# A message-passing layer on one core: nodes laid out in blocks of 49 to a partition, the list of edges packed in another order

## The chip, the cores and the metric

The kernel runs on one core of a Trainium2 chip. A core has five engines with an instruction queue each: TensorE (PE, matmuls; its weight loads are PEld), VectorE (DVE), ScalarE (ACT), GpSimd (POOL) and SyncE (SP, which issues DMAs). Transfers are carried by 16 DMA engines. They can be issued by SyncE and ScalarE, and by GpSimd where rows are gathered by an index. The metric is the time of one execution on the device in microseconds, lower is better.

## The reference

There are 6,250 nodes with 64 features each (`x`) and 206,250 edges sorted by their destination `dst`, each with a source node `src` and 64 features of its own (`edge_attr_64`).

```python
h = jnp.maximum(_layernorm(x, axis=-1), 0.0)
msg = h[src] + edge_attr_64
agg = jax.ops.segment_sum(msg, dst, num_segments=6250)
y = jax.nn.relu(agg @ W1 + b1) @ W2 + b2
return x + y
```

## The kernel before

**Two ways to sum over edges.** Of 202 tiles of 1,024 edges the rows of the first GA = G - GP = 178 are never gathered. For them the kernel counts how often source s occurs among the edges of each destination, and multiplies the normalized features `h` by these counts. A source is split into a low part, 0 to 127, and a high part, 0 to 48. A slot of three destinations holds up to 128 edges; `count` (L704) builds one-hot matrices `hot_lo` and `hot_key` on VectorE, one matmul (L720) makes the 128 x 147 counts, ScalarE writes them to SBUF (L722), and `product` (L750) multiplies them by `h3`, which is `h` in three bf16 parts (L755 for two of them, L758 for the third). Partition and column of `x` in SBUF (`xl`, L146) must match the low and high part of a source: `xl[lo, hi]` is the row of that node. The features of the edges themselves are summed by `chunk_sum` (L407), for all tiles but the last GP = 24. For these 24 tiles GpSimd gathers rows of `h` from a DRAM copy, `table`, adding them to the edges' features (`pfeat`), 8 gathers to a tile, and `sum_groups` (L440) sums both.

**The head of the program.** Instructions are issued in an order written out by hand (L134), so each engine runs them in the order of the text.

- x is loaded in three parts by SyncE (L151), then the last 106 rows (L152). Node n sits in partition n mod 128, column n // 128.
- The source list (L140) is made float by ScalarE (L242), turned by TensorE into rows of edges (`turn_src`, L245), and copied to `srcl` as integers. The list of destinations `dstn` is loaded by ScalarE's queue (L243).
- From every 256th destination (`firsts_i`, L138) comes for each slot the row of 256 edges in which it begins (`row_i`, L258). `fetch_row` (L275) gathers that row on GpSimd, four at a time in flight; `seek` (L279) finds the place in it on ScalarE; `place` (L285) makes the edge's number on VectorE.
- `norm_mean` (L461), `norm_center`, `norm_var` and `norm_root` are the layer norm on VectorE with squares on ScalarE, in three parts of 16, 16 and 17 columns.
- L561 packs destination and source into one word; L564 stores the list to DRAM (`packed`). `fetch_pair` (L541) gathers 129 words from there for each of 256 slots, `unpack` (L587) takes them apart, `turn` (L600) turns them into `keys`, from which counting starts.
- `norm_h` (L492) makes `h` and stores it to `table`. Row r of the table is lo * 49 + hi, so the sources of the last 24 tiles are converted by `table_rows` (L521), three instructions on VectorE.

**The main loop.** 22 blocks of 84 slots, 14 steps each. `before` (L894) names what is put in ahead of a step, besides counting and multiplying: the parts of `norm_b` and `norm_c` that finish `h3`, clearing of `sums`, further `fetch_row`, `seek` and `place`. `queue` and `pool_until` (L853) spread the gathers on GpSimd over the steps by a planned cost of each. After the loop (L1029 on) stand the last multiplications, the last groups of gathered tiles and the stores of `out_y`.

Of the kernel before, what the change touches and what calls it, by code (L numbers as in the profile page):

```python
# [9 lines left out]
F32 = mybir.dt.float32  # L10
BF16 = mybir.dt.bfloat16
I32 = mybir.dt.int32
I16 = mybir.dt.int16
AF = mybir.ActivationFunctionType
OP = mybir.AluOpType
# [92 lines left out]
def gnn_kernel(ctx: ExitStack, tc: tile.TileContext, x, src_t, dst_t, dst_g, edge, w1, b1, w2, b2, out):  # L108
# [31 lines left out]
    nc.scalar.dma_start(src, src_t[:, :GA * J])  # L140
    dstn = pr.tile([QA, 2, P * J], I32, name="dstn")

    firstp_i = small.tile([1, GP], I32, name="firstp_i")
    nc.scalar.dma_start(firstp_i.rearrange("o (q h k) -> o q h k", h=2, k=1),
                        dst_g[GA // 2:G // 2, :, 0:1].unsqueeze(0))
    xl = consts.tile([P, HI + 1, D], F32, tag="x", name="xl")  # L146
    nc.gpsimd.memset(xl[:, HI - 1, :], 0.0)
    thirds = [(0, 16), (16, 32), (32, HI)]
    for h0, h1 in thirds:
        h1 = min(h1, HI - 1)  # L150
        nc.sync.dma_start(xl[:, h0:h1, :], x[h0 * P:h1 * P, :].rearrange("(h l) d -> l h d", l=P))  # L151
    nc.sync.dma_start(xl[:N % P, HI - 1, :], x[N - N % P:, :])  # L152

# [59 lines left out]
    for q in range(JQ):  # L213
# [25 lines left out]
    nc.vector.tensor_tensor(less, rest.unsqueeze(2).to_broadcast([P, NR, P]),  # L239
                            iota_v.unsqueeze(1).to_broadcast([P, NR, P]), op=OP.is_lt)  # L240
    srcf = src.bitcast(F32)
    nc.scalar.activation(srcf, src, AF.Copy)  # L242
    nc.scalar.dma_start(dstn, dst_g[:QA])  # L243

    def turn_src(h):  # L245
        pt = ps.tile([P, J, P], F32, tag="pc", name="psrc")
        for j in range(J):
            nc.tensor.transpose(pt[:GA // 2, j, :], srcf.rearrange("p (q h j) -> p q h j", h=2, j=J)[:, :, h, j], ident)
        nc.scalar.activation(srcl[:GA // 2, h].rearrange("q p j -> q j p"), pt[:GA // 2], AF.Copy)

    turn_src(0)
    pf = ps.tile([P, IC], F32, tag="po", name="pf", bufs=1)
# [22 lines left out]
    def fetch_row(i):  # L275
        rows_of[i] = small.tile([P, L1], I32, name="rows", bufs=4)
        gather(rows_of[i], dst_g.rearrange("q h (r k) -> (q h r) k", k=L1), row_i[:, i:i + 1])

    def seek(i0, n):  # L279
        for i in range(i0, i0 + n):  # L280

            inrow = small.tile([P, L1], BF16, name="inrow", bufs=2)
            nc.scalar.activation(inrow, rows_of[i], AF.Sign, bias=nhalf[:, i:i + 1], accum_out=first[:, i, 1:2])  # L283

    def place(i0, n):  # L285
        to = first[:, i0:i0 + n, 0]
        nc.vector.scalar_tensor_tensor(to, first[:, i0:i0 + n, 1], -0.5, middle[:, i0:i0 + n],  # L287
                                       op0=OP.mult, op1=OP.add)
        nc.vector.tensor_scalar(first_i[:, i0:i0 + n], to, float(EA), None, op0=OP.min)
# [230 lines left out]

    def table_rows(index, tmp):  # L521

        nc.vector.tensor_scalar(tmp, index, LO_BITS, None, op0=OP.logical_shift_right)
        nc.vector.tensor_scalar(index, index, P - 1, None, op0=OP.bitwise_and)
        nc.vector.scalar_tensor_tensor(index, index, float(HI), tmp, op0=OP.mult, op1=OP.add)

    def find_groups():
# [18 lines left out]
    for i in range(4):  # L546
        fetch_row(i)
    turn_src(1)
    firstp = small.tile([1, GP], F32, name="firstp")
# [9 lines left out]
    norm_means()  # L559
    for h in range(2):  # L560
        nc.vector.scalar_tensor_tensor(dstn[:, h], dstn[:, h], DST_BITS,  # L561
                                       srcl[:QA, h].rearrange("q p j -> q (p j)"),
                                       op0=OP.logical_shift_left, op1=OP.bitwise_or)
    nc.scalar.dma_start(packed.rearrange("(q k) o -> q (k o)", q=QA), dstn.rearrange("q h k -> q (h k)"))  # L564
    seek(0, 3)
    for i in range(4, 7):
        fetch_row(i)
    place(0, 3)
    fetch_pair(0)
    for k in range(3):  # L570
        norm_center(k)
        if k < 2:
            seek(3 + 2 * k, 2)
    norm_var(0)
    norm_var(1)
    place(3, 4)
    fetch_pair(2)
    norm_var(2)
# [290 lines left out]
    chunk_starts(0, 2 * RC, "pc", 2)  # L869
    src_hi = late.tile([P, NWIN + NX], BF16, tag="part", name="src_hi").bitcast(I32)[:, :GP * J]  # L870
    table_rows(src_p, src_hi)
    unpack_pair(0)
# [18 lines left out]
    def then(k, f):  # L891
# [4 lines left out]
        2: [lambda: [fetch_h(g) for g in range(GA, GA + 4)], lambda: chunk_turn(0)],  # L896
        3: [lambda: open_pv(0, True), lambda: rows_later(7, 11)],
        16: [lambda: seek(9, 2), lambda: rows_later(11, IC)],
        18: [lambda: place(7, 4)],
        7: [lambda: norm_b(0)],  # L900
        9: [lambda: norm_b(1)],
        11: [lambda: norm_b(2)],
        15: [lambda: seek(7, 2), find_groups, lambda: norm_c(0), lambda: clear(0, 5)],
        17: [lambda: norm_c(1), lambda: clear(1, 5)],
# [180 lines left out]
    with tc.If(odd > 0):  # L1085
# [20 lines left out]
        with tc.For_i(0, G, 1) as g:  # L1106
# [6 lines left out]
            nc.sync.dma_start(index, src_t[:, ds(g * J, J)])  # L1113
            index_hi = work.tile([P, J], I32, name="index_hi", bufs=1)
            table_rows(index, index_hi)
            dst_1 = work.tile([P, J], I32, name="dst_1", bufs=1)
# [61 lines left out]
```

## Time and profile before

| | us |
|---|---|
| runs shown: median (lowest, highest) | 533.04 (532.72, 538.49) |
| the profiled execution | 525.21 |
| its span, first to last instruction | 523.4 |
| busy in the span: PE, PEld | 451.5, 385.6 |
| busy: DVE, ACT, POOL | 417.4, 360.1, 415.7 |
| mean granted TensorE clock | 0.974 |

The costliest groups of instructions (line, engine, operation, output and inputs, count; busy us, mean ns of one; idle time just before them and what ended it):

```profile
L267 POOL DMA_INDIRECT pfeat<-table,src_p x192 | 363.5, 1893 | 58.5 <-issue 54.9
L722 ACT ACTIVATE counts<-pc 128x882 bf16<-128x882 f32 x310 | 276.8, 908 | 41.0 <-PE pc L720 27.0
L720 PE MATMUL pc<-hot_key,hot_lo 128*128 128x147 bf16 x1860 | 175.1, 231 | 24.2 <-DVE hot_key L712 17.5
```

And the busy share of the DMA engines and what they moved, in 40 slices of 13.1 us:

```profile
DMA  9819812566577766654666676676577676676610
GB/s 203 211 42 329 220 29 39 146 172 156 117 171 179 167 171 181 171 138 95 161 162 155 149 178 153 140 184 163 129 173 175 137 198 146 141 192 164 155 14 14
```

A digit is a busy share in tenths. The first three slices are the head of the program: loads of x and of the lists in the first two, the steps between packing and counting in the third. Counting starts in the fourth. "Idle before" counts waiting ahead of a group; it costs time only on the engine that sets the end.

### The profile page before, as it was taken

How to read it: one execution, taken by the hardware profiler on the slowest of the kernel's cores; microseconds unless marked ns; L12 is line 12 of the kernel's file. 1: busy time of each engine (PE TensorE's matmuls, PEld its weight loads, DVE VectorE, ACT ScalarE, POOL GpSimd, SP SyncE). 2: the span in 40 equal slices, each digit the busy share in tenths (PEclk: the TensorE clock that was granted, in tenths of full speed). 3: DMA queues.
4: the chain of work that ended last, by engine and by line, in shares of the span. 5: the costliest groups of instructions: out<-in, count | busy, mean ns of one | idle time of the engine just before them, and what ended most of it. 6: DMA issues, size and time to landing. Idle time of an engine off the chain costs nothing. (4 is left out here: it accounts for less than half of the span.)

```text
span 523.4 us, 19099 instructions
## 1 busy us (share of the span) xinstructions
PE 451.5 (86%) x8183; PEld 385.6 (74%) x8184; DVE 417.4 (80%) x618; ACT 360.1 (69%) x534; POOL 415.7 (79%) x265
## 2 busy tenths in 40 slices
PE   3026767999699999988999999999999999999954
PEld 3015555888588888777888888888888888888743
DVE  5589986889699989988898978888879888879210
ACT  5246898778467767896777777777777777768300
POOL 6358888888888868888889888888888888888840
PEclk9999899999799999999999999999999999999977
DMA  9819812566577766654666676676577676676610
GB/s 203 211 42 329 220 29 39 146 172 156 117 171 179 167 171 181 171 138 95 161 162 155 149 178 153 140 184 163 129 173 175 137 198 146 141 192 164 155 14 14
DMA packets 118152, 78.78 MB, mean 151 GB/s; under 512 B 39096, under 2 KB 113326, under 8 KB 117870
## 3 DMA queue, kind: packets, MB, share of 16 engines
q1 hardware_dynamic: 88458, 64.95, 42.7%
q0 software_dynamic: 29200, 10.25, 16.7%
q10 hardware_dynamic: 404, 2.30, 1.5%
q8 instruction: 66, 1.08, 0.9%
q14 instruction: 24, 0.20, 0.1%
HBM read 73.48 MB, written 3.99 MB: 148 GB/s over the span
## 5 line engine op out<-in xcount | busy, mean ns | idle before, releaser
L267 POOL DMA_INDIRECT pfeat<-table,src_p x192 | 363.5, 1893 | 58.5 <-issue 54.9
L722 ACT ACTIVATE counts<-pc 128x882 bf16<-128x882 f32 x310 | 276.8, 908 | 41.0 <-PE pc L720 27.0
L720 PE MATMUL pc<-hot_key,hot_lo 128*128 128x147 bf16 x1860 | 175.1, 231 | 24.2 <-DVE hot_key L712 17.5
L712 DVE TENSOR_TENSOR hot_lo<-iota_lo,keys 128x1536 bf16<-128x1536 bf16 x155 | 148.0, 955 | 46.5 <-PE pc L720 46.0
L720 PEld LDWEIGHTS <-hot_lo 128*128 128x128 bf16 x1860 | 135.3, 100 | 47.7 <-DVE hot_key L712 22.3
L712 DVE TENSOR_TENSOR hot_key<-iota_key,keys 128x1776 bf16<-128x1776 bf16 x155 | 167.1, 1078 | 0.0
L755 PE MATMUL pv<-counts,h 128*128 128x252 bf16 (+1 forms) x1078 | 149.6, 273 | 0.1
L755 PEld LDWEIGHTS <-h 128*128 128x128 bf16 x1078 | 99.2, 98 | 8.7 <-issue 0.4
L758 PE MATMUL pv<-counts,h 128*64 128x252 bf16 (+1 forms) x1078 | 78.0, 280 | 0.0
L407 PE MATMUL bank<-feat,hot 128*21 128x64 f32 x3168 | 59.0, 223 | 1.5 <-DMA feat<-in_edge 0.8
L410 ACT ACTIVATE by_node<-bank 128x128 f32<-128x128 f32 x66 | 18.4, 278 | 60.8 <-PE bank L407 60.7
L758 PEld LDWEIGHTS <-h 128*64 128x64 bf16 x1078 | 55.3, 113 | 4.4 <-issue 0.8
L407 PEld LDWEIGHTS bank<-feat,hot 128*21 128x21 f32 x3168 | 47.4, 102 | 14.8 <-issue 9.5
L395 DVE TENSOR_TENSOR hot<-rel,iota 128x504 f32<-128x504 bf16 x66 | 44.6, 677 | 0.6 <-PE bank L407 0.6
L267 POOL DMA_INDIRECT rows<-in_dst_g,row_i x15 | 18.6, 1238 | 14.9 <-ACT inrow L283 7.9
L267 POOL DMA_INDIRECT words<-packed,first_i x15 | 19.5, 1302 | 4.6 <-issue 3.4
L419 PE MATMUL pv<-select,by_node 128*64 128x42 f32 x264 | 21.2, 244 | 0.4 <-ACT by_node L410 0.4
L419 PEld LDWEIGHTS pv<-select,by_node 128*64 128x64 f32 x264 | 13.2, 137 | 9.1 <-issue 1.1
L440 PE MATMUL bank<-hotp,pfeat 128*64 128x42 f32 x384 | 14.7, 233 | 5.5 <-DMA pfeat<-table,src_p 4.2
L440 PEld LDWEIGHTS bank<-hotp,pfeat 128*64 128x64 f32 x384 | 12.8, 138 | 8.3 <-DMA pfeat<-table,src_p 4.7
L767 DVE TENSOR_TENSOR sums<-sums,pv 128x252 f32<-128x252 f32 x22 | 9.0, 409 | 10.9 <-PE pv L758 10.9
L309 PE MATMUL pstart<-begins,first 128*1 128x9 f32 (+2 forms) x30 | 1.2, 172 | 19.0 <-DVE first L287 19.0
(171 smaller groups left out, 273.5 us busy)
## 6 DMA issues: line engine op xcount, KB each, us to landing
feat<-in_edge SPq DMA_DIRECT2D x132, 384.0 KB
pfeat<-in_edge SPq DMA_DIRECT2D x24, 256.0 KB
pfeat<-table,src_p POOLq DMA_INDIRECT x192
xl<-in_x SPq DMA_DIRECT2D x3, 512.0 KB
out_y<-y SPq DMA_DIRECT2D x24, 63.0 KB
xs<-in_x SPq DMA_DIRECT2D x4, 315.0 KB
table<-xl SPq DMA_DIRECT2D x2, 512.0 KB
dstn<-in_dst_g ACTq DMA_DIRECT2D x1, 768.0 KB
```

The costliest lines, as they stand in the source:

```text
L267: nc.gpsimd.indirect_dma_start(out=rows, out_offset=None, in_=source, in_offset=bass.IndirectOffsetOnAxis(ap=index, axis=0), compute_op=op)
L395: nc.vector.tensor_tensor(hot_of[u][:, :n].rearrange("p c j w -> p (c j) w"), rel[:, c:c + n].rearrange("p c q k -> p (c q k)").unsqueeze( ...
L407: nc.tensor.matmul(bank[q * QP:q * QP + WQ, i * D:(i + 1) * D], hot[:, i, j, :], feat[i][:, j, :], start=(k == 0), stop=(k == JP - 1))
L410: nc.scalar.activation(by_node[u][:, :n].rearrange("p c d -> p (c d)"), bank[:, :n * D], AF.Copy)
L419: nc.tensor.matmul(pvs[b][0][i * D:(i + 1) * D, a:a + CN], of[:, i, :], select, start=False, stop=False)
L440: nc.tensor.matmul(pa[k:k + D, b, :], tiles[b][:, j, :], hot[:, j, :], start=(j < 2), stop=(j >= J - 2))
L712: nc.vector.tensor_tensor(hot.rearrange("p t (m o) -> p t m o", o=2), iota_k.rearrange("p (m o) -> p m o", o=2).unsqueeze(1).to_broadcast( ...
L720: nc.tensor.matmul(pc[:, k, m * K:(m + 1) * K], hot_lo[:, j, :], hot_key[:, j, :K], start=True, stop=True)
L722: nc.scalar.activation(counts[b % 2][:, :, s * ST * V:(s + 1) * ST * V].rearrange("p h (k m) -> p h k m", k=2), pc[:, :, :ST // 2 * K].rea ...
L755: nc.tensor.matmul(pv, h3[:, h, :2 * D], of, start=(h == 0 and not clear), stop=False)
L758: nc.tensor.matmul(pv[k:k + D, :], h3[:, h, 2 * D:], of, start=False, stop=(h >= HI - 2))
L767: nc.vector.tensor_tensor(at[:, :BN], at[:, :BN], pv[:, o:], op=OP.add)
```

## The change

Node n is now in partition n // 49, column n mod 49. Partitions 0 to 126 hold 49 nodes each, partition 127 the last 27; its other columns are zeroed by GpSimd (from partition 96 on, before the loads). Each third of x is loaded by one DMA of 127 partitions, 16 or 17 rows of x in one run per partition. Row r of the table is then node r, and `table_rows` goes.

A source must now be split into lo = s // 49 and hi = s mod 49. ScalarE makes lo_f = s / 49 - 24/49 and 128 s; VectorE rounds lo_f to a whole number by adding and subtracting 1.5 * 2^23; then 128 (s - 49 lo) + lo is made in one instruction on VectorE. `lo_f` lies in a part of `counts0` that is not yet in use. `turn_src(0)` moves behind that, after the first four `fetch_row`.

Besides: `dstn` is loaded at the start; packing, fetching, seeking, centering and placing are interleaved differently; the packed list is stored by SyncE instead of ScalarE's queue; rows 7 to 10 are fetched before counting starts instead of from step 3 on, their seeks move from steps 15 and 16 to 4 and 5, their place from 18 to 8, and rows 11 to 14 are fetched from step 5 on instead of 16.

```diff
--- before.py
+++ after.py
@@ -139,17 +139,21 @@
     src = pr.tile([P, GA * J], I32, name="src")
     nc.scalar.dma_start(src, src_t[:, :GA * J])
     dstn = pr.tile([QA, 2, P * J], I32, name="dstn")
+    nc.scalar.dma_start(dstn, dst_g[:QA])
 
     firstp_i = small.tile([1, GP], I32, name="firstp_i")
     nc.scalar.dma_start(firstp_i.rearrange("o (q h k) -> o q h k", h=2, k=1),
                         dst_g[GA // 2:G // 2, :, 0:1].unsqueeze(0))
     xl = consts.tile([P, HI + 1, D], F32, tag="x", name="xl")
-    nc.gpsimd.memset(xl[:, HI - 1, :], 0.0)
+
+    NL = N // HI
+    assert NL == P - 1
     thirds = [(0, 16), (16, 32), (32, HI)]
+    nc.gpsimd.memset(xl[96:, N % HI:, :], 0.0)
     for h0, h1 in thirds:
-        h1 = min(h1, HI - 1)
-        nc.sync.dma_start(xl[:, h0:h1, :], x[h0 * P:h1 * P, :].rearrange("(h l) d -> l h d", l=P))
-    nc.sync.dma_start(xl[:N % P, HI - 1, :], x[N - N % P:, :])
+        nc.sync.dma_start(xl[:NL, h0:h1, :], x[:NL * HI, :].rearrange("(l h) d -> l h d", l=NL)[:, h0:h1, :])
+        if h0 == 0:
+            nc.sync.dma_start(xl[NL:, :N % HI, :], x[NL * HI:, :].unsqueeze(0))
 
 
     zero = small.tile([P, 1], F32, name="zero")
@@ -238,9 +242,13 @@
     less = pr.tile([P, NR, P], BF16, tag="less", name="less")
     nc.vector.tensor_tensor(less, rest.unsqueeze(2).to_broadcast([P, NR, P]),
                             iota_v.unsqueeze(1).to_broadcast([P, NR, P]), op=OP.is_lt)
+
+
+    lo_f = counts[0].rearrange("p h n -> p (h n)").bitcast(F32)[:, HI * D:HI * D + GA * J]
+    nc.scalar.activation(lo_f, src, AF.Copy, scale=1.0 / HI, bias=-(HI // 2) / HI)
     srcf = src.bitcast(F32)
-    nc.scalar.activation(srcf, src, AF.Copy)
-    nc.scalar.dma_start(dstn, dst_g[:QA])
+    nc.scalar.activation(srcf, src, AF.Copy, scale=float(P))
+    nc.vector.tensor_scalar(lo_f, lo_f, 1.5 * (1 << 23), 1.5 * (1 << 23), op0=OP.add, op1=OP.subtract)
 
     def turn_src(h):
         pt = ps.tile([P, J, P], F32, tag="pc", name="psrc")
@@ -248,7 +256,6 @@
             nc.tensor.transpose(pt[:GA // 2, j, :], srcf.rearrange("p (q h j) -> p q h j", h=2, j=J)[:, :, h, j], ident)
         nc.scalar.activation(srcl[:GA // 2, h].rearrange("q p j -> q j p"), pt[:GA // 2], AF.Copy)
 
-    turn_src(0)
     pf = ps.tile([P, IC], F32, tag="po", name="pf", bufs=1)
     for c in range(NR):
         nc.tensor.matmul(pf, minus, from_hw[:, c, :IC], start=(c == 0), stop=False)
@@ -518,12 +525,6 @@
     nc.sync.dma_start(src_p, src_t[:, GA * J:])
     nc.sync.dma_start(dst_p, dst_t.rearrange("p (g j) -> p g j", j=J)[:, GA:, :])
 
-    def table_rows(index, tmp):
-
-        nc.vector.tensor_scalar(tmp, index, LO_BITS, None, op0=OP.logical_shift_right)
-        nc.vector.tensor_scalar(index, index, P - 1, None, op0=OP.bitwise_and)
-        nc.vector.scalar_tensor_tensor(index, index, float(HI), tmp, op0=OP.mult, op1=OP.add)
-
     def find_groups():
 
         nc.vector.tensor_scalar(base_i[:, GA:], row2[0:1, GA:], 0.0, float(N - 1), op0=OP.max, op1=OP.min)
@@ -545,6 +546,8 @@
 
     for i in range(4):
         fetch_row(i)
+    nc.vector.scalar_tensor_tensor(srcf, lo_f, 1.0 - P * HI, srcf, op0=OP.mult, op1=OP.add)
+    turn_src(0)
     turn_src(1)
     firstp = small.tile([1, GP], F32, name="firstp")
     nc.vector.tensor_copy(firstp, firstp_i)
@@ -557,24 +560,33 @@
     for k in range(3):
         norm_mean(k)
     norm_means()
-    for h in range(2):
+
+    def pack(h):
         nc.vector.scalar_tensor_tensor(dstn[:, h], dstn[:, h], DST_BITS,
                                        srcl[:QA, h].rearrange("q p j -> q (p j)"),
                                        op0=OP.logical_shift_left, op1=OP.bitwise_or)
-    nc.scalar.dma_start(packed.rearrange("(q k) o -> q (k o)", q=QA), dstn.rearrange("q h k -> q (h k)"))
-    seek(0, 3)
-    for i in range(4, 7):
+
+    pack(0)
+    seek(0, 2)
+    fetch_row(4)
+    fetch_row(5)
+    norm_center(0)
+    pack(1)
+    nc.sync.dma_start(packed.rearrange("(q k) o -> q (k o)", q=QA), dstn.rearrange("q h k -> q (h k)"))
+    seek(2, 2)
+    norm_center(1)
+    place(0, 2)
+    fetch_pair(0)
+    fetch_row(6)
+    norm_center(2)
+    place(2, 2)
+    fetch_pair(2)
+    norm_var(0)
+    seek(4, 3)
+    norm_var(1)
+    place(4, 3)
+    for i in range(7, 11):
         fetch_row(i)
-    place(0, 3)
-    fetch_pair(0)
-    for k in range(3):
-        norm_center(k)
-        if k < 2:
-            seek(3 + 2 * k, 2)
-    norm_var(0)
-    norm_var(1)
-    place(3, 4)
-    fetch_pair(2)
     norm_var(2)
     norm_root()
     pools[0].__exit__(None, None, None)
@@ -867,8 +879,6 @@
     for g in range(GA, GA + 2):
         load_h(g)
     chunk_starts(0, 2 * RC, "pc", 2)
-    src_hi = late.tile([P, NWIN + NX], BF16, tag="part", name="src_hi").bitcast(I32)[:, :GP * J]
-    table_rows(src_p, src_hi)
     unpack_pair(0)
     chunk_rows(0, 2 * RC)
     chunk_columns(0, 2, "pc", 2)
@@ -894,13 +904,14 @@
     before = {
         1: [lambda: chunk_nodes(0)],
         2: [lambda: [fetch_h(g) for g in range(GA, GA + 4)], lambda: chunk_turn(0)],
-        3: [lambda: open_pv(0, True), lambda: rows_later(7, 11)],
-        16: [lambda: seek(9, 2), lambda: rows_later(11, IC)],
-        18: [lambda: place(7, 4)],
+        3: [lambda: open_pv(0, True)],
+        4: [lambda: seek(7, 2)],
+        5: [lambda: seek(9, 2), lambda: rows_later(11, IC)],
+        8: [lambda: place(7, 4)],
         7: [lambda: norm_b(0)],
         9: [lambda: norm_b(1)],
         11: [lambda: norm_b(2)],
-        15: [lambda: seek(7, 2), find_groups, lambda: norm_c(0), lambda: clear(0, 5)],
+        15: [find_groups, lambda: norm_c(0), lambda: clear(0, 5)],
         17: [lambda: norm_c(1), lambda: clear(1, 5)],
         19: [lambda: norm_c(2), lambda: clear(2, 5)],
         21: [lambda: clear(3, 5)],
...
```

The part left out is the same removal of `table_rows` in a branch that these inputs do not enter.

More of the change, by code (lines that the diff above doesn't have):

```diff
@@ L1113, in gnn_kernel @@
             nc.sync.dma_start(index, src_t[:, ds(g * J, J)])
-            index_hi = work.tile([P, J], I32, name="index_hi", bufs=1)
-            table_rows(index, index_hi)
             dst_1 = work.tile([P, J], I32, name="dst_1", bufs=1)
```

## The prediction

> **What bounds the kernel now.** I read the page first, then the chain of waits, then the timeline and table of stretches for the two ends.
>
> The chain of work that ended last comes first, because it names who sets the end:
>
> ```profile
> 503.03 3.56 DMA pfeat<-table,src_p
> 506.59 0.04 issue
> 506.63 0.45 PE bank L440 x2
> ...
> 509.03 1.05 PE pv L755 x5
> 510.08 2.03 PE pv L758 x18
> ```
>
> The end hangs on the last indirect gather of node rows. GpSimd issues 192 of them back to back, and TensorE stands waiting for the last ones: its last group pair begins at 500.58 us, could be done at about 501.8, and ends at 507.07. So TensorE is 5.2 us ahead of GpSimd. In between, TensorE is the bound (144.49 of 150 us busy from 150 to 300, 149.53 of 150 from 300 to 450). Whatever moves the first counting step therefore moves everything behind it.
>
> The head of the program is next: VectorE's timeline.
>
> ```profile
> 17.67 1.29 DVE L463 TENSOR_REDUCE stat<-xl 128x17 f32<-128x1088 f32 x1 [2.71 <-DMA xl<-in_x]
> 18.99 0.19 DVE L466 TENSOR_SCALAR stat<-stat 128x49 f32<-128x49 f32 x1
> 19.09 2.35 DVE L561 SCALAR_TENSOR_TENSOR dstn<-dstn,srcl 96x1024 int32<-96x1024 int32 x2
> ...
> 33.06 0.17 DVE L583 TENSOR_SCALAR nbase<-nfirst 128x15 f32<-128x15 f32 x1
> 33.14 0.25 DVE L523 TENSOR_SCALAR src_hi<-src_p 128x192 int32<-128x192 int32 x1
> ...
> 34.00 0.29 DVE L591 TENSOR_SCALAR klo<-words 128x256 int32<-128x256 int32 x1
> ```
>
> VectorE runs in order. The three row sums of x stand ahead of the packing of the list, and the last of them waits for the last third of x until 17.67. From packing hang the store of the list, its gather and the first unpacking, which starts at 34.00; the first counting matmul follows at 42.89. So the landing of x (call it L = 17.67) is on the path, and 16.3 us lie between it and unpacking.
>
> Last, two transfers near the end, where nothing else moves, in the table of stretches (behind the clock: share of the 16 DMA engines busy, GB/s). At 515.34 VectorE finishes rows of 101 partitions, at 517.81 rows of 126; each is stored by SyncE as 512 B a partition.
>
> ```profile
> 515.34 0.29 DVE L825 TENSOR_TENSOR y<-y,xs 101x128 f32<-101x128 f32 x1
> 517.81 0.29 DVE L825 TENSOR_TENSOR y<-y,xs 126x128 f32<-126x128 f32 x1 [2.19 <-ACT y L820]
> ```
>
> ```profile
> 516.50:518.20 1.70, 0.67 (x4) 0.54 (x4) 0.29 (x1) 0.52 (x2) 0.00 (x0) 1.00 0.07 21
> 518.80:519.40 0.60, 0.00 (x0) 0.00 (x0) 0.00 (x0) 0.00 (x0) 0.00 (x0) 1.00 0.38 101
> 3.30:4.20 0.90, 0.00 (x0) 0.00 (x0) 0.56 (x1) 0.82 (x2) 0.86 (x6) 1.00 1.02 424
> ```
>
> The store of 101 partitions runs at a share of 0.07, one sixteenth, and 21 GB/s: one DMA engine of sixteen carries all 51.7 KB, for 2.4 us. The store of 126 runs at 101 GB/s. The third line is the load of the source list, 128 partitions of 5.7 KB: all engines, 424 GB/s, 26.5 GB/s each. 101 is prime, and so is 127, the number of partitions in each new load of x.
>
> **The load of x: the step that decides.** Now: 2,048 runs of 256 B per third, 219 GB/s between 12.0 and 14.9, in by 17.67. After: 127 runs of 4,096 B (the last third 4,352 B). The runs are better, the division is not. The row of 101 partitions says one engine. What that row cannot say is whether the three loads would share that engine. The Trainium skill, page "DMA: Bandwidth & Descriptors", section "Why a DMA increments its semaphore by 16 and not by 1", does: the number of engines is the largest up to 16 that divides the outer size of both sides, 127 partitions give 1, and the lowest-numbered engines are the ones used. So the three loads queue behind each other on the first engine. By the trace alone (one engine each, perhaps different ones) L would be about 29; by the rule about 71.
>
> Working: 127 x 49 x 256 B = 1.593 MB. The first engine also takes its sixteenth of the destination list (48 KB) and of six row gathers (48 KB), and the 7 KB of partition 127: 1.697 MB. At 26.1 GB/s (between 418 and 437 GB/s over 16, slices around the source list) that is 65.0 us. x starts at about 4.9, when the 1,024 four-byte reads ahead of it on SyncE's queue are through (56 GB/s at a share of 1.28 in 4.5 to 4.8). With 0.8 us for the last receipt L = 70.7. This is **53.0 us later**. Bounds: 27.3 GB/s (437/16) gives L = 67.9; 21 GB/s, the row of the store with its 512 B runs, gives 86.5. I take 26.1 because the runs of 4 KB are nearer to 5.7 KB.
>
> **From L to the first unpacking, new order.** Third sum and scale 1.42 (17.67 to 19.09); pack 1.2; centering 1.2 (L470, 3.55 for three); pack 1.2; so the store of the list leaves at L + 5.1. Before, it was issued at 21.48 and its traffic had ebbed by 25.9; I take L + 9.3 for its landing (bounds L + 8.5, and L + 12.0 from 28.42 - 21.48). Two word gathers at 1.25 with their gaps; then row 6, issued at L + 11.8, landing 1.9 after its issue ends (28.11 to 30.01): L + 14.65. ScalarE's seek 0.6, place 0.4, the third variance 1.3, two small ones 0.2: unpacking at L + 17.25. Now 16.33, in which the three removed operations of table_rows (33.14 to 34.00) are 0.9. So the new chain is **0.9 us longer**: place(4, 3) makes VectorE wait for row 6, behind which the third variance is queued. First unpacking at 88.0 instead of 34.0.
>
> **What comes back.** Rows 7 to 10 (43.95 to 50.02 on GpSimd, 6.1 us) move ahead of fetch_dst, where GpSimd idles 4.53 us waiting for VectorE. The first gather of node rows is then held by the table's store, about 10.2 us behind unpacking instead of 16.0. GpSimd gains 5.8 on TensorE: the 5.2 us of waiting at the end go. That wait also drops the granted clock to 0.50 from 504 to 512; the 7.0 us of matmuls from 508.0 to 515.0 would be about 5.2 at full clock. And at 71.00 TensorE waits 2.15 for VectorE, held by place(7, 4) behind ScalarE's seeks; these go to steps 4 to 8, where VectorE has no idle time (3.00 of 3.00). Of these last two (1.8 and at most 2.15, against four seeks, 2.7 us of ScalarE, put in elsewhere) I count 1.3. Together **-6.5** (bounds 0 and -9).
>
> **Edits costed at nothing**, all over long before 70 us: a second ScalarE pass over the sources (1.39 as L242), VectorE's rounding of 1,424 columns (0.9 by L592's slope of 0.5 ns an element, or 1.6 by L561's 1.04; I take 0.9) and combination (1.6), turn_src behind them (transposes 2.0 and copies 2.0 each); ready at about 17.8. The longer memset, 1.5 us by the slope from 64 to 128 columns (0.15, 0.21), ends before row_i at 9.4. dstn earlier on ScalarE's queue delays only firstp_i, first read near 11.6. The packed store on SyncE waits for VectorE; behind it stand the loads of pfeat, feat and the table stores, which need later work anyway. If x came early, this cover would be gone, and the list's own chain (source columns turned by 17.8, second pack by 19.7) would count.
>
> **Sum.** 53.0 + 0.9 - 6.5 = +47.4 us on the profiled execution: 525.2 (span 523.4 and 1.8 around it) becomes 572.6. The runs shown have a median of 533.0, 7.8 above it; the delay is a fixed one at the start, so I add it there: 580.4.
>
> **Rivals.**
> 1. *The load is spread over all engines after all.* The store of 101 partitions is a store, the change a load, and no load of a prime number of partitions stands alone in this trace; that speaks for it. Against: the same queue and form. At 350 GB/s x and dstn (2.38 MB) are in by about 13, the list's chain decides: packed stored at 19.8, landing 24.0, row 6 29.3, unpacking near 32.0, 2.0 earlier. With -6.5: 516.7, or 524.5 by the median. It decides where L is below 23.3 (17.67 + 6.5 - 0.9), that is from 1.6 MB in 18 us, 87 GB/s, between three and four engines.
> 2. *One engine for each load, but different ones.* L = 4.9 + 20.2 + about 3.7 shared + 0.3 = 29: +11.4 + 0.9 - 6.5 = +5.8, 538.9 by the median. Against it: only the skill's sentence on the lowest-numbered engine.
> 3. *One engine, as slow as the 512 B row:* L = 86.5, +63 - 6.5: 590; with nothing coming back at the end, 596.
>
> **How the numbers follow.** The queueing on one engine 0.86 (rival 3 is its upper part), the spread load 0.08, separate engines 0.06. Its own range is 564 to 602: 27.3 GB/s with all 9 us back gives 574 and a little more overlap less; 21 GB/s with the store's late landing and nothing back gives 600. That holds about 0.8 of everything, so the range is not widened to the small cases. This kernel can't be told from no change within about 1%: faster 0.08, within 1% 0.03 (half of the separate engines), slower 0.89.
>
> **What would show it.** In the slices from 10 to 70 us DMA at a share near 0.06 and 26 GB/s with every engine nearly idle; L463's last sum waiting for x some 55 us; first matmul of L720 near 97 instead of 42.89; then a program that runs as before, without L440's waits for pfeat at the end and with a full clock there. Wrong it is if x comes in at over 100 GB/s.

## The result, and the profile after

The changed kernel is slower by about an eighth.

| | before | after |
|---|---|---|
| median (lowest, highest), 4 runs each on one chip | 535.01 (532.72, 538.49) | 600.86 (598.95, 602.77) |
| ratio, 95% interval | | 1.1225 (1.1141 to 1.1308) |
| profiled execution, its span | 525.21, 523.4 | 598.95, 597.3 |
| third row sum of x starts (L) | 17.67 | 72.69 |
| first unpacking starts | 34.00 | 91.54 |
| first counting matmul | 42.89 | 100.43 |

So the first counting matmul is 57.5 us later, and the median is 65.85 us higher. The other 8.3 us are lost behind it.

The page of the changed kernel, its DMA rows in 40 slices of 14.9 us and the group of the row sums (count; busy us, mean ns; idle time before them and what ended it):

```profile
DMA  4200136821556567666555676756666566666540
GB/s 114 75 26 30 40 110 200 254 67 16 130 131 166 131 165 190 142 177 159 144 130 124 150 179 138 167 139 153 135 177 162 128 141 177 154 156 139 134 113 13
...
L470 DVE TENSOR_REDUCE stat<-xl 128x16 f32<-128x1024 f32 (+1 forms) x3 | 3.7, 1242 | 55.4 <-DMA xl<-in_x 55.4
```

The third and fourth slice (30 to 60 us) have digit 0 at 26 and 30 GB/s: 15 engines of 16 have nothing to do. VectorE waits 55.4 us for x in all.

The table of stretches says it exactly (length; busy us and count of PE, PEld, DVE, ACT, POOL; then the clock, the share of the 16 DMA engines and GB/s):

```profile
30.00:35.00 5.00, 0.00 (x0) 0.00 (x0) 1.22 (x1) 0.00 (x0) 0.00 (x0) 1.00 0.06 26
45.00:50.00 5.00, 0.00 (x0) 0.00 (x0) 0.00 (x0) 0.00 (x0) 0.00 (x0) 1.00 0.06 26
```

A share of 0.06 is one sixteenth. In the second stretch no engine computes anything.

VectorE's timeline of the changed kernel (start, us; idle time before it and what ended it):

```profile
8.96 0.17 DVE L232 CAST firsts<-firsts_i 128x8 f32<-128x8 int32 x1 [5.10 <-DMA firsts_i<-in_dst_g]
...
31.25 1.22 DVE L470 TENSOR_REDUCE stat<-xl 128x16 f32<-128x1024 f32 x1 [16.42 <-DMA xl<-in_x]
51.20 1.22 DVE L470 TENSOR_REDUCE stat<-xl 128x16 f32<-128x1024 f32 x1 [18.74 <-DMA xl<-in_x]
72.69 1.29 DVE L470 TENSOR_REDUCE stat<-xl 128x17 f32<-128x1088 f32 x1 [20.27 <-DMA xl<-in_x]
...
91.54 0.28 DVE L603 TENSOR_SCALAR klo<-words 128x256 int32<-128x256 int32 x1
```

The three loads come in one behind the other: 127 x 4,096 B = 520,192 B in the 19.95 us between the first two sums is 26.1 GB/s, and 127 x 4,352 B in the next 21.49 is 25.7. They share one engine, not one each: SyncE had issued the third load by 37.46 us (its timeline stands in the last section), and with an engine of its own that load would have been in near 59, not at 72.69. The first line matters too: the first destinations are in at 8.96, where before they were in at 5.77.

And at the end of the program, TensorE's timeline of the changed kernel:

```profile
582.68 1.13 PE L447 MATMUL bank<-hotp,pfeat 128*64 128x42 f32 x32 [0.37 <-ACT sum_p L450]
...
585.85 1.16 PE L770 MATMUL pv<-counts,h 128*64 128x252 bf16 x18
```

The last group of gathered tiles waits 0.37 us for ScalarE and not for `pfeat`, and the granted clock is 1.00 from 582 to 592 us. The wait at the end that bounded the profiled execution of before is gone, as forecast, and yet what stands behind the first count is longer. That is what most of the experiments are about.

### The profile page after: what moved, and what is told of

Its sections match the earlier page's. It is cut to its first block, busy times and chain, and to the rows that moved or that the text cites. A ratio compares the mean times of both kernels' runs of the same rounds, so it can differ in the third digit from the quotient of the medians.

```text
span 597.3 us, 19097 instructions
## 1 busy us (share of the span) xinstructions
PE 461.8 (77%) x8183; PEld 388.6 (65%) x8184; DVE 418.7 (70%) x619; ACT 354.3 (59%) x535; POOL 428.6 (72%) x265
## 4 chain that ended last, share of the span: by engine, by line
PE 67%; DMA 10%; ACT 8%; DVE 4%; another core or an unknown queue 4%; issue 3%; SPq 2%; POOL 0%; ACTq 0%; DVEq 0%; POOLq 0%
PE pc L732 21%; PE pv L767 16%; PE bank L414 10%; PE pv L770 10%; DMA xl<-in_x 6%; ACT counts L734 4%; PE pv L426 3%; SPq L156 2%; PE ph L823 2%; PE bank L447 2%; PE po L830 2%; DMA dstq<-in_dst_g,cols_i 2%; DMA feat<-in_edge 1%; DMA packed<-dstn 1%
## 5 line engine op out<-in xcount | busy, mean ns | idle before, releaser
L274 POOL DMA_INDIRECT pfeat<-table,src_p x192 | 376.4, 1961 | 64.1 <-issue 54.2
L734 ACT ACTIVATE counts<-pc 128x882 bf16<-128x882 f32 x310 | 273.8, 909 | 35.5 <-PE pc L732 23.2
L732 PE MATMUL pc<-hot_key,hot_lo 128*128 128x147 bf16 x1860 | 177.2, 232 | 22.8 <-DVE hot_key L724 11.6
L767 PE MATMUL pv<-counts,h 128*128 128x252 bf16 (+1 forms) x1078 | 151.7, 275 | 0.4 <-issue 0.3
L767 PEld LDWEIGHTS <-h 128*128 128x128 bf16 x1078 | 100.4, 99 | 9.8 <-issue 0.6
L770 PE MATMUL pv<-counts,h 128*64 128x252 bf16 (+1 forms) x1078 | 76.6, 275 | 0.8 <-issue 0.8
L414 PE MATMUL bank<-feat,hot 128*21 128x64 f32 x3168 | 67.3, 223 | 7.6 <-issue 4.6
L417 ACT ACTIVATE by_node<-bank 128x128 f32<-128x128 f32 x66 | 18.4, 278 | 89.7 <-PE bank L414 56.2
L414 PEld LDWEIGHTS bank<-feat,hot 128*21 128x21 f32 x3168 | 50.2, 102 | 21.5 <-issue 16.4
L470 DVE TENSOR_REDUCE stat<-xl 128x16 f32<-128x1024 f32 (+1 forms) x3 | 3.7, 1242 | 55.4 <-DMA xl<-in_x 55.4
L480 ACT ACTIVATE counts<-xl 128x1024 f32<-128x1024 f32 (+1 forms) x3 | 3.2, 1074 | 55.3 <-DVE xl L477 55.0
L274 POOL DMA_INDIRECT rows<-in_dst_g,row_i x15 | 17.6, 1172 | 10.7 <-DVE nhalf L271 4.8
```

The source lines that it names most:

```text
L274: nc.gpsimd.indirect_dma_start(out=rows, out_offset=None, in_=source, in_offset=bass.IndirectOffsetOnAxis(ap=index, axis=0), compute_op=op)
L414: nc.tensor.matmul(bank[q * QP:q * QP + WQ, i * D:(i + 1) * D], hot[:, i, j, :], feat[i][:, j, :], start=(k == 0), stop=(k == JP - 1))
L417: nc.scalar.activation(by_node[u][:, :n].rearrange("p c d -> p (c d)"), bank[:, :n * D], AF.Copy)
L732: nc.tensor.matmul(pc[:, k, m * K:(m + 1) * K], hot_lo[:, j, :], hot_key[:, j, :K], start=True, stop=True)
L734: nc.scalar.activation(counts[b % 2][:, :, s * ST * V:(s + 1) * ST * V].rearrange("p h (k m) -> p h k m", k=2), pc[:, :, :ST // 2 * K].rea ...
L767: nc.tensor.matmul(pv, h3[:, h, :2 * D], of, start=(h == 0 and not clear), stop=False)
```

## The experiments

Twelve kernels were run, in four groups. The chips differ: the kernel before had a median of 535.48 in the first group, 524.05 in the second, 535.14 in the third and 537.99 in the fourth. So times are compared within a group alone, and from group to group only ratios, and steps of the loop are counted from each kernel's own first counting step.

| kernel | what differs | us | ratio to before (95%) | first counting matmul |
|---|---|---|---|---|
| x_112 | after, x as 112 + 15 partitions | 544.96 | 1.0162 (1.0085 to 1.0239) | 44.44 |
| x_124 | after, x as 124 + 3 | 555.47, one run | | 55.90 |
| x_122 | after, x as 122 + 5 | 564.03, one run | | 69.09 |
| b_127 | before, x as 127 + 1 | 615.12, one run | | 123.00 |
| b_again | before | 521.08, one run | | 42.86 |
| b_rows | before with the rows' move alone | 531.77 | 1.0161 (1.0076 to 1.0246) | 42.99 |
| x_112_rows | x_112 without the rows' move | 527.33 | 1.0053 (1.0022 to 1.0085) | 44.56 |
| x_112_dst | x_112 with dstn loaded late | 530.27 | 1.0145 (1.0068 to 1.0222) | 41.64 |
| b_rows_q | b_rows, second dstq gather earlier | 539.13 | 1.0074 (1.0046 to 1.0102) | 43.30 |
| x_112_dst_q | x_112_dst, the same | 540.10 | 1.0102 (1.0037 to 1.0168) | 42.59 |
| x_112_rows_dst | x_112 without the rows' move and with dstn late | 534.22 | 0.9996 (0.9967 to 1.0024) | 42.78 |
| a_rows | after without the rows' move | 594.88 | 1.1077 (1.1023 to 1.1132) | 100.57 |

The "rows' move" is the earlier fetching of rows 7 to 10, with their seeks and their place.

### Is it the number of partitions? (x_112, x_124, x_122, b_127)

The first three cut each load of x in two, so that the greater part has 112, 124 or 122 partitions. Nothing else changes, neither the runs of 4 KB nor the placing of nodes.

```diff
-        nc.sync.dma_start(xl[:NL, h0:h1, :], x[:NL * HI, :].rearrange("(l h) d -> l h d", l=NL)[:, h0:h1, :])
+        for l0, l1 in ((0, 112), (112, NL)):
+            nc.sync.dma_start(xl[l0:l1, h0:h1, :],
+                              x[l0 * HI:l1 * HI, :].rearrange("(l h) d -> l h d", l=l1 - l0)[:, h0:h1, :])
```

The fourth puts 127 partitions into the kernel before, which has runs of 256 B and the old placing.

```diff
-        nc.sync.dma_start(xl[:, h0:h1, :], x[h0 * P:h1 * P, :].rearrange("(h l) d -> l h d", l=P))
+        for l0, l1 in ((0, 127), (127, P)):
+            nc.sync.dma_start(xl[l0:l1, h0:h1, :], x[h0 * P:h1 * P, :].rearrange("(h l) d -> l h d", l=P)[l0:l1])
```

What was expected of x_112:

> The changed kernel, but each third of x is loaded by two DMAs, of 112 and 15 partitions instead of one of 127. Same bytes, same 4 KB runs, same order of everything else. If the number of partitions puts the load on one engine (theory), these two go to 16 and 15 engines: the last sum of x starts near 15 us instead of 72.69, unpacking near 35 (then held by the list's own chain), and the time falls by about 56 us from 600.9, to 535 to 545. If the layout or the runs of 4 KB are what is slow, or the other edits (rival), x still lands near 70 and the time stays at 600.

of x_124:

> As the run with 112 and 15, but cut into 124 and 3. 124 is divisible by 4 and by no larger number up to 16. Theory of the largest divisor: four engines, 104 GB/s, 15 us for x; it starts near 10 as in the changed kernel, so the last sum of x starts near 26, and the time lies about 46 us below 600.9, near 555. If instead any number that is not a multiple of 16 falls back to one engine, it stays at 600.

of x_122:

> Cut into 122 and 5. 122 is 2 times 61: two engines, 52 GB/s, 30 us for x, last sum near 42, the time near 571. If any number that is no multiple of 16 takes one engine: 600.

and of b_127:

> The kernel before with its own layout and its runs of 256 B, and nothing changed but that each third of x is loaded by a DMA of 127 partitions and one of 1. Theory: one engine, and with runs of 256 B at 219/16 = 13.7 GB/s; 1.56 MB take 114 us, the last sum starts near 120 and the time is about 100 us above before, near 637. If another edit makes the changed kernel slow (rival), this stays at 535.

VectorE's timeline of x_112, at the lines that were 31.25 to 72.69 above:

```profile
15.17 3.53 DVE L472 TENSOR_REDUCE stat<-xl 128x16 f32<-128x1024 f32 x3
...
35.55 0.28 DVE L605 TENSOR_SCALAR klo<-words 128x256 int32<-128x256 int32 x1
```

The same of x_124:

```profile
21.01 1.22 DVE L472 TENSOR_REDUCE stat<-xl 128x16 f32<-128x1024 f32 x1 [5.14 <-DMA xl<-in_x]
28.16 1.29 DVE L472 TENSOR_REDUCE stat<-xl 128x17 f32<-128x1088 f32 x1 [5.92 <-DMA xl<-in_x]
```

The same of x_122:

```profile
30.89 1.22 DVE L472 TENSOR_REDUCE stat<-xl 128x16 f32<-128x1024 f32 x1 [10.58 <-DMA xl<-in_x]
41.45 1.29 DVE L472 TENSOR_REDUCE stat<-xl 128x17 f32<-128x1088 f32 x1 [9.33 <-DMA xl<-in_x]
```

And of b_127:

```profile
68.66 1.22 DVE L464 TENSOR_REDUCE stat<-xl 128x16 f32<-128x1024 f32 x1 [27.47 <-DMA xl<-in_x]
97.88 1.29 DVE L464 TENSOR_REDUCE stat<-xl 128x17 f32<-128x1088 f32 x1 [28.00 <-DMA xl<-in_x]
```

Read them by the distance of the last two sums. 124 partitions: 124 x 4,352 B in 7.15 us is 75 GB/s. 122: 122 x 4,352 B in 10.56 is 50 GB/s. 127, in the changed kernel: 26. 112 + 15: the three sums stand in one row without a wait. That is the order of the rule cited in the prediction (the Trainium skill, page "DMA: Bandwidth & Descriptors", section "Why a DMA increments its semaphore by 16 and not by 1"), which gives 4, 2, 1 and 16 engines. Between 124 and 127 partitions lie 44.5 us of L, and bytes, runs and order are the same. The last sums had been expected near 26 for 124 partitions and near 42 for 122, and came at 28.16 and 41.45. And b_127 carries the delay over to a kernel that has nothing else of the change: its first counting matmul moves from 42.89 to 123.00. There the engine is even slower, 18.1 GB/s (520,192 B in the 28.69 us between the first sum, at 39.97, and the second), with runs of 256 B; it had been put lower still beforehand, 13.7, which is why 615.12 came out below the 637 expected. That the load spreads whatever the number of partitions (the prediction's rival 1) is refuted.

But x_112 is not faster than before, though its x is early. Its sums stand at 15.17, its unpacking at 35.55, 1.55 us later than before, and it takes 1.6% longer (interval 0.85% to 2.4%). So something else of the change costs time.

### What else costs: the rows' move and the early list (b_again, b_rows, x_112_rows, x_112_dst)

b_again is the kernel before once more, to see whether its profiled execution had been an odd one. b_rows is before with one part of the change alone, the earlier fetching of rows 7 to 10:

```diff
     fetch_pair(2)
+    for i in range(7, 11):
+        fetch_row(i)
...
-        3: [lambda: open_pv(0, True), lambda: rows_later(7, 11)],
-        16: [lambda: seek(9, 2), lambda: rows_later(11, IC)],
-        18: [lambda: place(7, 4)],
+        3: [lambda: open_pv(0, True)],
+        4: [lambda: seek(7, 2)],
+        5: [lambda: seek(9, 2), lambda: rows_later(11, IC)],
+        8: [lambda: place(7, 4)],
...
-        15: [lambda: seek(7, 2), find_groups, lambda: norm_c(0), lambda: clear(0, 5)],
+        15: [find_groups, lambda: norm_c(0), lambda: clear(0, 5)],
```

x_112_rows is x_112 with this undone. x_112_dst is x_112 with the load of `dstn` put back behind ScalarE's pass over the sources:

```diff
     dstn = pr.tile([QA, 2, P * J], I32, name="dstn")
-    nc.scalar.dma_start(dstn, dst_g[:QA])
...
     nc.scalar.activation(srcf, src, AF.Copy, scale=float(P))
+    nc.scalar.dma_start(dstn, dst_g[:QA])
```

What was expected of b_again:

> The kernel before, unchanged, for a second profile. The prediction took back 6.5 us at the end from a profile whose own time, 525.2, is below every other run of this kernel (532.6 to 539.2). Theory: in an ordinary execution TensorE is about 10 us slower through the loop, so GpSimd is no longer late at the end: first count to last about 456 us as in the run with 127 partitions, no wait of TensorE for pfeat at the end, and nothing to be taken back. Rival: the waits for pfeat at the end (5.2 us) stand in this one too.

of b_rows:

> The kernel before with one part of the change alone: rows 7 to 10 fetched ahead of the loop, their seeks at steps 4 and 5, their place at 8, rows 11 to 14 from step 5. By the prediction's sum this gains 5 to 6.5 us (529 to 530). If GpSimd is not late at the end in an ordinary execution, it gains nothing (535); if this move is what makes the loop of the changed kernels 9 us longer than that of the run with 127 partitions, it loses 5 to 9 (540 to 544).

of x_112_rows:

> The changed kernel with x in 112 and 15 partitions, and with that same move undone. If the move makes the loop longer, this falls from 545 to 536 to 540. If the loss sits in another part (layout, the other order of the head, planner's places for the gathered groups), it stays at 545; by the prediction's sum it would rise to 550.

and of x_112_dst:

> The changed kernel with x in 112 and 15 partitions, and the list of destinations loaded where it was before, behind ScalarE's two passes over the sources. The firsts (1,024 reads of 4 bytes on SyncE's queue) landed at 5.8 before and at 9.4 with the change. If it is the early list that holds them up, they land near 6 again, row_i and everything behind it come 3 us earlier, first count near 41.3 instead of 44.4, time near 542. If it is the larger runs of x on the same queue that hold them, nothing moves.

b_again did not show what was expected of it: TensorE's waits for `pfeat` stand in it too, 4.4 us. It ran on a chip where before has a median of 524.05, so it says nothing yet of a chip with a median of 535; that comes with a_rows.

The move alone makes the kernel before slower, 1.0161, and undoing it in x_112 takes 1.0162 down to 1.0053 (two chips, so this is a comparison of ratios). It was to give time back. It does so at first: b_rows reaches step 40 at 59.45 us after its first counting step, b_again at 62.03. Then it loses 13.2 us in one place, between steps 60 and 80 (from 86.27 to 130.46, against 88.79 to 119.77).

GpSimd's and VectorE's timelines of b_rows there:

```profile
63.66 11.12 POOL L267 DMA_INDIRECT pfeat<-table,src_p  x1 [0.30 <-issue]
...
73.37 0.43 DVE L598 TENSOR_TENSOR khif<-khi,nbase 128x258 f32<-128x258 int32 x1
...
138.51 0.95 POOL L267 DMA_INDIRECT dstq<-in_dst_g,cols_i  x1 [0.30 <-issue]
...
141.54 0.42 DVE L352 TENSOR_SCALAR dstq<-dstq,cols 128x384 f32<-128x384 int32 x1 [11.58 <-DMA dstq<-in_dst_g,cols_i]
```

The same of b_again:

```profile
64.59 4.18 POOL L267 DMA_INDIRECT pfeat<-table,src_p  x1 [0.30 <-issue]
...
68.90 0.17 DVE L287 SCALAR_TENSOR_TENSOR first<-first,middle 128x4 f32<-128x4 f32 x1 [1.55 <-ACT inrow L283]
...
127.83 1.53 POOL L267 DMA_INDIRECT dstq<-in_dst_g,cols_i  x1 [0.30 <-issue]
...
132.42 0.53 DVE L352 TENSOR_SCALAR dstq<-dstq,cols 128x384 f32<-128x384 int32 x1 [0.15 <-DMA dstq<-in_dst_g,cols_i]
```

The rows that go ahead put gathers of node rows in front of another gather, `dstq`, which is queued at step 54 for use at step 62. In b_again it is issued at 127.83 and lands just in time, a wait of 0.15. In b_rows it is issued 10.7 us later, and VectorE waits 11.58 us for it, with counting queued behind. Part of the delay is one gather that holds GpSimd for 11.12 us. The DMA engines are not busy in that time, but VectorE is, without a gap, as this stretch of b_rows shows (VectorE 4.00 of 4.00 us; DMA share 0.02, 4 GB/s):

```profile
68.00:72.00 4.00, 3.14 (x37) 2.63 (x34) 4.00 (x6) 3.87 (x5) 4.00 (x1) 1.00 0.02 4
```

The end of that gather goes with VectorE's first pause. In b_rows VectorE has worked without a pause up to 73.34, and `khif` at 73.37 is the first instruction behind one; the gather ends at 74.78. In b_again VectorE is idle from 67.36, waiting for a seek on ScalarE (the 1.55 us at 68.90), and the gather ends at 68.77. In all fourteen traces, before and after included, this gather ends 1.42 to 1.45 us after VectorE's first pause since it began, whether it lasted 2.16 us (x_124 and x_122, which have a pause of 0.25 us close behind its start), 4.18 (the kernels without the move) or 9.49 to 11.13 (the other six with it). The move takes away the wait for that seek, and with it the pause. This is a reading of traces: no kernel with a pause put in was run, and other gathers pass at their usual length beside a VectorE that never pauses, so the pause is not all there is to it.

The list's early load costs something too. x_112_dst, VectorE's first line and TensorE's first counting matmul:

```profile
5.77 0.22 DVE L233 CAST firsts<-firsts_i 128x8 f32<-128x8 int32 x1 [1.91 <-DMA firsts_i<-in_dst_g]
...
41.64 1.66 PE L734 MATMUL pc<-hot_key,hot_lo 128*128 128x147 bf16 x12 [4.67 <-DVE hot_key L726]
```

In x_112, with `dstn` early, these are 9.39 and 44.44. So the 786 KB of the list on ScalarE's queue hold up the 1,024 four-byte reads on SyncE's queue by 3.6 us, and the first count by 2.8 (by 1.8 between x_112_rows and x_112_rows_dst, which differ in the same load). The total of x_112_dst (1.0145) can't be told from that of x_112 by its interval; it has a wait for `dstq` like that of b_rows (11.62 us, where x_112 has 2.5 in all).

### Is it the late gather alone? (b_rows_q, x_112_dst_q, x_112_rows_dst)

The first two queue the gather of `dstq` ten steps earlier; the third has neither the rows' move nor the early list.

```diff
-        before.setdefault(n, []).append(lambda t=t: queue.insert(0, (GATHER_US, lambda: fetch_dst(t))))
+        before.setdefault(n - (10 if t == 1 else 0), []).append(lambda t=t: queue.insert(0, (GATHER_US, lambda: fetch_dst(t))))
```

What was expected of b_rows_q:

> The kernel before with the row move alone (which made it 1.6% slower), and the second gather of destinations (dstq, read by chunk_nodes at step 62) put at the head of GpSimd's queue at step 44 instead of 54. Theory A: the whole loss is VectorE's wait of 11.6 us for that gather, late because more gathers of node rows were queued ahead of it and one of them held GpSimd 11.1 us. Then the wait goes and what is left is the gain of the move in steps 16 to 40 (2.5 us): ratio to before 0.990 to 0.995. Theory B: GpSimd itself is late by then (gather 16 at 59.0 us after the first count instead of 53.7), and as it sets the end the loss stays: 1.010.

of x_112_dst_q:

> The changed kernel with x in 112 and 15 partitions, the list of destinations loaded late, and the same gather at step 44. First count at 41.6 instead of 42.9 of before. Theory A: ratio to before 0.990 to 0.995, where the same kernel without the earlier gather had 1.0145. Theory B: 1.008.

and of x_112_rows_dst:

> The changed kernel with x in 112 and 15 partitions, the row move undone and the list of destinations loaded late: what is left of the change are the layout, the removed table_rows, the other order of the head and SyncE's store. With the row move undone alone the ratio was 1.0053 with a first count 1.7 us later than before; now it should come 1.2 earlier, and as the loop is the same, the ratio should be 0.998 (525 - 2.9 - ...: 523). If the loop is not the same (rival), it stays above 1.003.

The wait is gone in b_rows_q: 0.5 us in its table of waits. (In x_112_dst_q 3.6 us of it are left.) Its ratio is 1.0074, where b_rows had 1.0161, and 1 lies outside its interval. So the late gather is not the whole cost: theory A, with ratios below 1, is refuted. How much of the cost it is stays open, because the two ran on different chips and their intervals overlap. Theory B had put the figure near what was measured (1.010), but its reason is not in the trace: TensorE does not wait for `pfeat` at the end of b_rows_q. x_112_dst_q misses in the same way (1.0102). x_112_rows_dst behaves as expected: with 16 engines for x, and without the move and the early list, the new placing of nodes is worth nothing and costs nothing (0.9996). No version beat the kernel before.

### The same in the changed kernel itself (a_rows)

The changed kernel as it is, x in one load of 127, with only the move undone (the reverse of the diff of b_rows).

What was expected of it:

> The changed kernel with the move of rows 7 to 10 undone and nothing else (x still in one load of 127 partitions per third). Theory (the row move costs the rest of the program about 8 us, and the late first count of 57.5 us is all that x costs): first counting matmul near 100.4 as in the changed kernel, 535.1 + 57.5 = 592.6 where the kernel before takes 535.1, ratio 1.107; on a chip where the kernel before takes 524, 581.5, ratio 1.110. Prediction's sum (the row move gives 6.5 back): undoing it makes the kernel slower, about 607, ratio 1.135. Rival (the move costs only where x comes early, so it is without effect behind a late x): as the changed kernel, ratio 1.1225.

It takes 594.88, a ratio of 1.1077, where 1.107 was expected: 56.9 us above before, and its first counting matmul is at 100.57, 57.7 later. The late x accounts for all that is left, and nothing comes back from elsewhere. The move costs the rest, from 1.1077 to 1.1225, about 8 us; the two intervals do not overlap (1.1023 to 1.1132, 1.1141 to 1.1308).

This run also bears on why the wait at the end gave nothing back. The table of waits of b_again, on the faster chip, has (sum us, count, longest):

```profile
PE bank L440 <- DMA pfeat<-table,src_p: 4.4, 3, 1.6
```

and that of a_rows, on a slower one, in which GpSimd's gathers after the head are in the same order:

```profile
PE bank L414 <- issue: 4.2, 17, 0.4
...
PE bank L447 <- DMA pfeat<-table,src_p: 0.7, 1, 0.7
```

The groups of TensorE show the difference, b_again first:

```profile
L407 PE MATMUL bank<-feat,hot 128*21 128x64 f32 x3168 | 58.8, 223 | 1.5 <-DVE hot L395 0.8 <-DMA feat<-in_edge 0.8
```

then a_rows:

```profile
L414 PE MATMUL bank<-feat,hot 128*21 128x64 f32 x3168 | 66.8, 223 | 7.5 <-issue 4.2 <-DMA feat<-in_edge 1.9 <-DVE hot L402 0.7
```

The same 3,168 matmuls of the same 223 ns each take 58.8 us of TensorE on one chip and 66.8 on the other, with 6.0 us more idle time before them: 14 us, about what the medians of before differ by (524 to 535 or 538). The granted clock does not order them: 0.941 in b_again, 0.913 in a_rows, but 0.983 in the changed kernel, which has 67.3 us in this group. The profiled execution of before (525.21, 59.0 us in this group) is like the faster chip. Where TensorE is so much slower, it hardly waits for GpSimd at the end, with the move or without it: 2.0 us in b_127, 0.7 in a_rows, none in x_112_rows_dst or in the changed kernel. On the faster chip it does, again with the move or without it: 4.2, 4.4 and 7.8 in before, b_again and x_112_rows, and 4.3 and 2.4 in b_rows and x_112_dst, which have the move. So what took the wait away was the slower TensorE, not the move.

## Why the prediction was right, and which step was wrong

Its course was right: one DMA engine carries all three loads, L moves by 55 us, and everything behind moves with it. The size was too small: 600.86 against 580.4, or +65.85 us against the forecast +47.4. Of the 18.4 us missed, 3.6 lie ahead of the first count and 14.8 behind it. That 600.86 still falls inside the forecast range, 564 to 602, at its very top, is partly luck: the top was meant for an engine at 21 GB/s with nothing coming back, and what came was an engine at 26 with a loss behind it. By its own steps:

- **The load of x.** L was 72.69 against 70.7. The rate, 26.1 GB/s, was right (26.1 and 25.7). Most of the 2.0 us come in ahead of it: the first sum is at 31.25, where the forecast's own terms give 29.6. The four-byte reads in front of x were through 3.2 us later than before, and the prediction said that the early list "delays only firstp_i". x_112_dst shows that delay by itself; that it is what x lost was not tried.
- **From L to the first unpacking.** 18.85 against 17.25. The list's store was given L + 9.3 for its landing; the words are gathered at 83.81, L + 11.1, inside the bounds given (to L + 12.0) but not at the value chosen. a_rows repeats it (18.73).
- **First counting matmul.** Forecast 42.89 + 53.9, near 97; measured 100.43. Of the 3.6 us missed, 2.0 and 1.6 are the two above.
- **"What comes back", -6.5, is the step that failed.** Its sign was wrong: behind the first count the program lost 8.3 us. 5.2 of its 6.5 rested on TensorE's wait at the end, which executions on chips with such a median show at 0 to 2.0 us: it was read from an execution 7.8 us faster than the median it was taken from. With the move undone, 57.7 us at the start become 56.9 at the end, so there was next to nothing to be given back. And the move, which was to supply the gain ("GpSimd gains 5.8 on TensorE"), costs some 8 us. Even on the faster chip, where the wait exists, b_rows keeps 4.3 us of it, and its gather 16 comes 59.0 us after the first count instead of 53.7: GpSimd is 5.3 us later, not 5.8 earlier. The move does bring the earlier steps forward (2.6 us by step 40), but the prediction followed rows 7 to 10 on GpSimd only up to `fetch_dst` and the first gather of node rows. It did not follow it to the gather that is then held for 11 us, nor to the next one queued with just enough lead, the second `dstq`. That chain is seen in b_rows; in the changed kernel the wait for `dstq` is only 2.0 us, and what makes up the 8 us there is open (below).
- **Adding the delay to the median** was right: 535.1 + 57.5 = 592.6, ratio 1.107, is what a_rows shows.
- **Edits costed at nothing.** The sources on VectorE, the second pass of ScalarE, turn_src and the store on SyncE cost nothing here, behind a late x. With an early x they also cost nothing that can be told (x_112_rows_dst, 0.9996); only the list's early load does (1.8 to 2.8 us to the first count).
- **Rivals.** The spread load was given 524.5, a gain. x_112 makes the load spread and is 1.6% slower than before, so its sum was wrong by the same term and the early list. Separate engines are refuted by the sums' distances of 19.95 and 21.49 us. An engine at 21 GB/s is refuted by the 26. The sum for it does not come out either: from 17.67 to 86.5 are 68.8 us, not 63, so its own terms give about 596 with the 6.5 taken back and 603 without, and the range should have ended some 6 us higher.

**What stays open.** Why the early gather waits for a pause of VectorE when others do not; that a pause ends it is seen in every trace and not tried. What the move's 8 us are in the changed kernel: its steps 40 to 60 take 33.4 us against 29.6 in a_rows, and steps 60 to 309 another 3.5, with waits of VectorE for `dstq` of only 2.0 in all. In steps 40 to 60 one wait of VectorE stands out, 4.79 us up to 169.32, during which TensorE's matmuls come in small groups with "issue" before them; but x_112_rows_dst, without the move, has such a wait too (3.1 us). The long gather alone is not the answer: from the first count to the last, x_124 and x_122 take 466.1 and 463.6 us without it, the changed kernel 465.1 with it, a_rows 458.1. And what makes the `feat` matmuls slower to issue on some chips.

## What to carry to other kernels

Look at the number of partitions of a transfer before its run length: here 127, a prime, left it one DMA engine, and cutting the same load into 112 and 15 partitions brought the others back. A gather that is moved ahead can be paid for by the next just-in-time gather on that queue (11.6 us in b_rows), so follow the queue to there, not only to the first one that gains. And before slack at the end of a profile is booked as a gain, ask whether the execution it was read from is as fast as the median that the gain is taken from.

## What the hardware showed that was not expected

- SyncE itself stands while one engine works its loads off. The changed kernel's timeline of SyncE (issue of the DMAs, us each):

```profile
2.17 12.93 SPq L156 DMA_DIRECT2D xl<-in_x  x1
15.15 22.31 SPq L154 DMA_DIRECT2D xl<-in_x  x2
37.51 20.53 SPq L516 DMA_DIRECT2D w1s<-in_w  x1
```

The load of `w1s`, 32 KB that have nothing to do with x, holds the issuing engine for 20.53 us (again 20.53 in a_rows; 0.52 in x_112, where x is spread, and 0.95 before). In b_127 it is the loads of x themselves, six issues in 93.29 us. Here nothing else waits for SyncE at that time; something urgent issued behind such a load would have been late too.

- One engine's rate went with the run: 26.1 GB/s with runs of 4 KB and 18.1 with runs of 256 B, both loads into 127 partitions. With runs of 4 KB, several engines came to less than a multiple of 26.1: 75 to 80 GB/s on what the rule says are four engines, 42 to 50 on two.
- A transfer of large runs on one queue delays small reads on another: 1,024 reads of four bytes landed at 9.39 instead of 5.77 when 786 KB in runs of 8 KB were issued on the other queue at the same time (x_112 against x_112_dst).
- A gather issued by GpSimd can stand for up to 11.13 us beside a VectorE that works without a pause, and end 1.42 to 1.45 us after the first pause, with the DMA engines at a share of 0.02 (b_rows). This is seen in one gather of each of the fourteen traces; it was not tested by an experiment.
